# Two adaLN layers on one core: the opening's loads and gate clamps, one rotation in the overlap of the layers, and the loads of the first large feed-forward weights, each put at another place in the order of work

## The chip, the cores and the metric

One core of a Trainium2 chip runs the whole program. The metric is the device time of one execution in microseconds (us). The kernel before was timed in three runs: 1821.15, 1821.19 and 1821.67, median 1821.19. One more execution was profiled.

The names of the profile: PE is TensorE (the matrix products), PEld the loading of its weights, DVE is VectorE, ACT is ScalarE, POOL is GpSimd, SP is SyncE, which here only issues transfers (DMAs). SPq and POOLq rows are DMA issues of those engines. PEclk or "clock" is the share of full speed that TensorE was granted.

## The reference

Eight batches of 512 tokens with 256 features go through two layers. Each layer draws six vectors per batch from a small input c, and uses them to scale and shift a layer norm ahead of an attention and ahead of a feed-forward block, and to gate what is added back:

```python
def layer(x, c, wmod, attn, ffn):                    # twice: L0 and L1
    sa, ca, ga, sb, cb, gb = split6(silu(c) @ wmod)  # per batch, 256 each
    ga = (2 * (ga >= 0) - 1) * maximum(abs(ga), 0.25)   # "clamp"
    gb = (2 * (gb >= 0) - 1) * maximum(abs(gb), 0.25)
    x = x + ga * attn(layernorm(x) * (1 + ca) + sa)
    x = x + gb * ffn(layernorm(x) * (1 + cb) + sb)
    return x

def L0_attn(x):      # 16 heads of 16
    h = rmsnorm(x) * norm_w
    q, k, v = h @ Wq, h @ Wk, h @ Wv
    lin = causal linear attention on taylor(q @ Wqf), taylor(k @ Wkf), v
    win = softmax attention in a window of 64 keys on q, k, v
    return x + concat(lin, win) @ Wout

def L0_ffn(x):
    xr, xk = mixes of x and the token before it (mu_r, mu_k)
    return sigmoid(xr @ W_r) * (square(relu(xk @ W_k)) @ W_v)

def L1_attn(x):      # 16 heads of 16, causal softmax
    Q, K, V = split(x @ w_qkv); Q, K = rope(Q), rope(K)
    return softmax(causal(Q @ K.T / 4)) @ V @ w_proj + b_proj

def L1_ffn(x):       # w1, w2, h1, h2, w3: ternary weights (-1, 0, 1), a scale per output
    h = silu(x @ w1 * s) * (x @ w2 * s)              # 256 -> 1024
    h = gelu(h @ h1 * s); h = gelu(h @ h2 * s)       # 1024 -> 1024, twice
    return h @ w3 * s                                # 1024 -> 256
```

## The kernel before

**The order of the work.** For everything up to the feed-forward block of layer 1 the order is written out by hand. Each piece of work is a small function, entered in a plan with a time by `when(time, what)` (layer 0) or `when1(time, what)` (attention of layer 1). The plan is sorted by time, and the pieces issue their instructions in that order, each to the queue of its own engine; an engine works through its queue in order. So a piece's time sets its place in the queues and nothing else: it waits there until its inputs and its memory are ready, and all that stands behind it on that engine waits too. The unit of time in layer 0 is a step; a batch has 20 steps, and steps from 169 on (the last attention steps and the block after them) count for 0.8. In layer 1 a step counts for 0.603 from its tenth on, and its first falls at 160.6 of layer 0's scale: this stretch, in which the last batches of layer 0 and the first scores of layer 1 stand side by side in the plan, is called the overlap here. Pieces with a negative time are the opening.

**The opening (lines 150 to 310, and 924 to 937).** SP issues the loads: the two c's, x of batch 0, the three slices of layer 0's modulation weights (wm), then Wq, Wk, Wv, wqf, wkf, normw, then layer 1's wm and the rest. `on_every_row` (L228) makes, by products with a c that is spread over all rows (L226), the rows 1+ca, sa and ga for batch 0, all in one PSUM tile; the modulation on DVE (L409, L411) reads the first two, a clamp (L214 to 220) the third. `by_batches` (L235) makes the rows of all batches, `kept_batches` (L246) adds 1 or clamps them, and writes them to `mod_dram`, from where each later batch fetches its rows (`mod_rows`, L124; `fetch_rows`, L386). `mod_features` (L258) makes those of the six vectors that are needed by feature (L266, products with 8 columns), and six DVE instructions copy them out (L271). `folded` (L187) multiplies Wq by Wqf's blocks and Wk by Wkf's, beginning with two transposes on PE (L191). POOL scales Wq, Wk and Wv by normw (L308), and fills constant tiles (memsets, L299 to 310). Batch 0 itself: statistics (L348), `root` and `better` (L327 and L333, the reciprocal root), norm (L364), modulation, sums of squares (L429), a second root, hr (L437), transposes (L452), projections to q and k (L103), products with the folded weights (L467), q's and k's parts (L474 to 487), and the first scores (L545).

**Layer 0 per batch.** Linear scores, window scores, values (L678, L693) and row sums; `finish(b)` (L748) makes the output projection and the feed-forward block. `keys(c)` (L848) projects for one half of the features, and `squared(c)` (L851) takes relu on ACT (L859) into a tile "relu" with the tag "rot" (all but the last batch), and multiplies on DVE into ka (L860).

**Layer 1's first q and k (`rotation`, L1097).** For batch 0 they are made in the overlap, for each of k and q in two chunks of 128 features: `projected` (PE, L103 in the profile's row of such products), `copied` (ACT, to "flat"), `swapped` (DVE, a stream shuffle into a tile "rot", the tag that relu has too), `rotated` three times (POOL, L1119), and `apart` twice (ACT, L1126), which writes the two parts that the scores read. The times stand in a table (L1143 to L1148).

**The feed-forward block of layer 1.** The last pieces of the plan are `gated(f)` and `gate_parts(f, i)` for f from 0 to 7, for batch 0: products (L1454), silu on ACT (L1466), row on DVE (L1469), and a split of row into two parts gh (DVE, L132) and gl (POOL, L133; DVE for the last f). Row has two buffers. Then the program loads a flag and branches: `feed_forward(True)` (L1485) runs if all weights are exactly ternary, which they are here. It opens its own memory pools and issues on POOL sixteen loads (h1 and h2, eight slices of 512 KB each, L1503 to L1507) and one of w3. The large products (L1543) run in groups of 16 per f and batch, 128 x 512 each. Its order within the branch is set by the scheduler of the framework, not by the plan.

**Pools.** The tiles of layer 0 and 1 come from pools with fixed tags and numbers of buffers (`fm`, `atp`, `tok`, `rp`, `wp`; PSUM: `sc`, `mm`). A pool that is closed gives its memory back, and a tile placed there later waits for those that used it.

Of the kernel before, what the change touches and what calls it, by code (L numbers as in the profile page):

```python
# [8 lines left out]
FP = mybir.dt.float32  # L9
BF = mybir.dt.bfloat16  # L10
FR = mybir.dt.float32r
# [6 lines left out]
P = 128  # L18
# [9 lines left out]
PAD = (24, 32)  # L28
# [8 lines left out]
def adaln_two_layers_kernel(ctx: ExitStack, tc: tile.TileContext, t, out):  # L37
# [100 lines left out]
    with ExitStack() as lctx:  # L138
# [3 lines left out]
        atp = lctx.enter_context(tc.tile_pool(name="at0", bufs=2))  # L142
# [10 lines left out]
        xs0, sT, wm = {}, [], []  # L153
        cs = [load(rp, f"c{i}", [P, NC, B], t[f"L{i}_cT"].rearrange("(k p) b -> p k b", p=P)) for i in range(2)]
        xs0[0] = tok.tile([P, NTB, D], FP, name="x", tag="x", bufs=4)
        nc.sync.dma_start(out=xs0[0], in_=t["L0_attn_x"][0].rearrange("(j p) d -> p j d", p=P))
# [14 lines left out]
        wq, wk, wv = (wqkv0[:, :, i * D : (i + 1) * D] for i in range(3))  # L171
        for w, name in ((wq, "L0_attn_Wq"), (wk, "L0_attn_Wk"), (wv, "L0_attn_Wv")):
# [3 lines left out]
        normw = load(rp, "normw", [P, NC], t["norm_w_cols"])  # L176
# [51 lines left out]
        def on_every_row():  # L228

            ps = got0["bc"] = sc.tile([P, 2, T], FP, name="sc", tag="sc")  # L230
            for o, v in ((D, 1), (0, 0)):
                mod_product(ps[:, 0, o : o + D], s_all, 0, v * D, D)
            mod_product(ps[:, 1, :D], s_all, 0, 2 * D, D)
# [12 lines left out]
        def kept_batches(layer, i=1):  # L246
            ps = got0["rows"]
            if i == 0:
                nc.vector.tensor_scalar_add(mod_a[:, 0, :], ps[:B, 0, D:], 1.0)
                nc.vector.tensor_copy(mod_a[:, 1, :], ps[:B, 0, :D])  # L250
            elif layer == 0:
                clamp(mod_a[:, 2:4, :].rearrange("p v d -> p (v d)"), ps[:B, 1, :])
                nc.sync.dma_start(out=mod_dram[:, 0:4, :], in_=mod_a)
            else:
                clamp(mod_b, ps[:B])
                nc.sync.dma_start(out=mod_dram[:, 4:6, :], in_=mod_b.rearrange("p (v d) -> p v d", d=D))

        def mod_features(i):  # L258
            if i == 0:
                got0["f"] = sc.tile([P, 2, T], FP, name="sc", tag="sc")  # L260
            psf = got0["f"][:, 0, : 6 * NC * B].rearrange("p (v c b) -> p v c b", v=6, c=NC)
            layer, v = ((0, 3), (0, 4), (1, 0), (1, 1), (1, 3), (1, 4))[i]
            for c in range(NC):
                w, o = wm[layer][v // 2], v % 2 * D + c * P
                for k in range(NC):
                    nc.tensor.matmul(  # L266
                        psf[:, i, c, :], w[:, k, o : o + P], sT[layer][:, k, :], start=(k == 0), stop=(k == NC - 1)
                    )
            if i == 5:
                for i in range(6):  # L270
                    nc.vector.tensor_scalar_add(modf[:, i], psf[:, i], float(i % 2))  # L271
# [46 lines left out]
        def when(time, what):  # L318
            plan.append((min(time, END0) + STEP0 * max(time - END0, 0.0), len(plan), what))
# [53 lines left out]
        def prepare(b):  # L373
# [3 lines left out]
            def fetch():  # L377
                if b == 0:
                    got0["ga"] = held["bc"] = rp.tile([P, 3, D], FP, name="bc", tag="bc")
                    return  # L380
                xs0[b] = tok.tile([P, NTB, D], FP, name="x", tag="x", bufs=4)
                nc.sync.dma_start(out=xs0[b], in_=t["L0_attn_x"][b].rearrange("(j p) d -> p j d", p=P))
                if b > 1:
                    fetch_rows()

            def fetch_rows():  # L386
                held["bc"] = mod_rows(rp, b, 0, 3, 1)

            when(t0 - 24.5, fetch)
            if b == 1:  # L390
                when(t0 - 22.7, fetch_rows)
# [3 lines left out]
                [t0 - 21.3 + 0.3 * j for j in range(NTB)],  # L395
                t0 - 20.25,
                [t0 - 17.85 + 0.4 * j for j in range(NTB)],
# [3 lines left out]
            row = lambda i: bcast(held["bc"][:, i, :], [P, NTB, D], 1)  # L401
# [74 lines left out]
            def apart(c, which, e):  # L476
                if e == 0:
                    ready[b, c, which] = fm.tile(
                        [P, 2, T], FP, name="q" + which, tag="q" + which, bufs=3 if which == "k" else 2
                    )  # L480
# [462 lines left out]
        def bring(i):  # L943
# [24 lines left out]
            else:  # L968
# [10 lines left out]
                fpool.tile([P, PAD[0]], FP, name="pad0", tag="pad0")  # L979
# [49 lines left out]
        def prepare1(b):  # L1029
# [67 lines left out]
            def rotation(c, which, in_time, at, then, turn, last):  # L1097
# [46 lines left out]
            for c, which, at, begin, then, turn, last in (  # L1144
# [340 lines left out]
    def feed_forward(exact):  # L1485
# [3 lines left out]
        with ExitStack() as fctx:  # L1489
# [6 lines left out]
            if exact:  # L1496
                tok.tile([P, PAD[1]], FP, name="pad1", tag="pad1", bufs=1)
            hp = fctx.enter_context(tc.tile_pool(name=f"hw{exact}", bufs=1 if exact else 3))
            mm = fctx.enter_context(tc.tile_pool(name=f"mm2{exact}", bufs=8, space=PSUM))

            if exact:
                h1 = hp.tile([P, NF, DH], FR, name="h1", tag="h1")
                for dst, name in ((h1, "h1T"), (h2, "h2T")):  # L1503
                    src = t[name].rearrange("(k p) n -> p k n", p=P)
                    for k in range(NF):
                        nc.gpsimd.dma_start(out=dst[:, k, :], in_=src[:, k, :])
                nc.gpsimd.dma_start(out=w3, in_=t["w3T"].rearrange("(k p) n -> p k n", p=P))  # L1507
                full.update(h1T=h1, h2T=h2)
# [187 lines left out]
```

## Time and profile before

| what | us |
|---|---|
| runs, median of 3 | 1821.19 |
| the profiled execution | 1825.46 |
| its span, first to last instruction | 1823.7 |
| PE busy | 1755.0 (96%) |
| DVE busy | 1073.2 (59%) |
| ACT busy | 883.8 (48%) |
| POOL busy | 720.6 (40%) |
| first product on PE | at 7.73 |
| first scores of layer 0 (L545) | at 33.74 |
| first large product (L1543) | at 1177.74 |

How to read it: the profiled execution took 4.27 us more than the median run, 1.76 us of it ahead of or behind the span. Times in the trace are from the span's start. A row of the timeline reads: start, duration, engine, line, operation, output<-inputs, shape, count of instructions that were put together, and in brackets the idle time of the engine before it with what ended it. A row of the waits reads: the waiting engine and line, `<-`, the engine and line that it waited for, total us, count, longest.

Where PE waits longest, by that reading: 7.73 at the start for the first slice of wm; 1.28 at 20.98 for hr; 0.78 at 35.64 and 2.36 at 53.77 behind DVE; 1.22 at 650.74 and 2.39 at 654.79 behind DVE; 1.06 at 677.00 behind ACT; and 7.20 at 1177.74.

### The profile page before, as it was taken

The page shows a single profiled execution, that of the slowest core. Times are in us where ns is not written, and L with a number is a line of the kernel's source. Part 1 is how long each engine was busy: PE and PEld are TensorE (multiplying, and loading weights), DVE is VectorE, ACT ScalarE, POOL GpSimd, SP SyncE. Part 2 cuts the span into 40 slices and gives each one's busy share as a digit, 9 for nine tenths or more (in the row PEclk, how much of TensorE's full clock was granted, in tenths as well). Part 3 has the DMA queues.
Part 4 walks back from the last instruction along what each step waited for, and adds up shares of the span by engine and source line. Part 5 has one row for each costly group of instructions (what it writes and reads, how often), then busy time and mean ns, then how long its engine had stood idle before and what let it go on. Part 6 is the DMA issues. An engine that isn't in the chain of part 4 may idle for free. (4 is left out here: it accounts for less than half of the span.)

```text
span 1823.7 us, 41142 instructions
## 1 busy us (share of the span) xinstructions
PE 1755.0 (96%) x16886; PEld 1200.6 (66%) x16886; DVE 1073.2 (59%) x3712; ACT 883.8 (48%) x1273; POOL 720.6 (40%) x1098
## 2 busy tenths in 40 slices
PE   7899999999999989999999999899999999999998
PEld 4456666665666655544555455588888888888887
DVE  5555574756656556578888887336353554636352
ACT  2766666766667645566666665323221222313221
POOL 4675766768575763456655554400000000000000
PEclk8999999999999999999999999999999999999999
DMA  4100101010001101023121111330000000000000
GB/s 151 37 14 6 37 5 37 5 38 21 24 17 34 40 4 39 1 65 116 50 74 56 56 49 37 122 115 27 1 27 11 17 27 1 27 1 27 0 12 14
DMA packets 42853, 65.59 MB, mean 36 GB/s; under 512 B 4112, under 2 KB 33424, under 8 KB 42656
## 3 DMA queue, kind: packets, MB, share of 16 engines
q1 hardware_dynamic: 37472, 46.62, 8.1%
q0 software_dynamic: 5184, 16.25, 3.0%
q8 instruction: 134, 2.20, 0.5%
q14 instruction: 63, 0.52, 0.1%
HBM read 50.24 MB, written 12.63 MB: 34 GB/s over the span
## 5 line engine op out<-in xcount | busy, mean ns | idle before, releaser
L1543 PE MATMUL mm<-gh,h 128*128 128x512 f32 x1024 | 398.7, 391 | 7.2 <-issue 7.2
L1543 PE MATMUL mm<-gl,h 128*128 128x512 f32 x1024 | 397.9, 390 | 0.0
L1205 DVE CUSTOM_DVE_ANT_0 junk<-sc,cmask 128x256 bf16<-128x256 f32 (+3 forms) x512 | 225.0, 486 | 93.7 <-PE sc L1194 93.3
L132 DVE CAST gh<-row 128x512 fp32r<-128x512 f32 x192 | 80.7, 424 | 265.3 <-ACT row L1589 128.8
L1263 ACT ACTIVATE at<-sc 128x768 f32<-128x768 f32 (+1 forms) x192 | 168.6, 880 | 116.2 <-PE sc L1194 103.0
L1543 PEld LDWEIGHTS mm<-gh,h 128*128 128x128 f32 x1024 | 193.1, 189 | 47.6 <-issue 7.6
L1543 PEld LDWEIGHTS mm<-gl,h 128*128 128x128 f32 x1024 | 193.1, 189 | 40.0
L642 POOL TENSOR_SCALAR_AFFINE_SELECT aw<-aw 64x512 f32<-64x512 f32 (+1 forms) x320 | 168.1, 552 | 101.3 <-ACT aw L632 95.3
L556 ACT ACTIVATE at<-sc 128x768 f32<-128x768 f32 (+1 forms) x192 | 163.9, 883 | 69.3 <-PE sc L545 68.7
L1194 PE MATMUL sc<-k,q 32*128 32x512 f32 (+3 forms) x1024 | 192.6, 473 | 2.2 <-ACT at L1263 2.1
L1252 PE MATMUL sc<-qs,k 32*128 32x384 f32 (+3 forms) x1024 | 190.2, 472 | 1.7 <-DVE qs L1236 1.7
L1267 POOL TENSOR_SCALAR_AFFINE_SELECT at<-at 128x256 f32<-128x256 f32 x256 | 102.9, 414 | 187.5 <-ACT at L1263 187.0
L589 DVE CUSTOM_DVE_ANT_0 junk<-sc,wmask 128x128 bf16<-128x128 f32 x512 | 115.3, 285 | 84.1 <-PE sc L578 84.0
L560 POOL TENSOR_SCALAR_AFFINE_SELECT at<-at 128x256 f32<-128x256 f32 x256 | 103.4, 424 | 112.7 <-ACT at L556 111.8
L1595 ACT ACTIVATE row<-mm,h_s_cols 128x512 f32<-128x512 f32 x64 | 44.0, 687 | 194.7 <-PE mm L1543 191.5
L133 DVE TENSOR_TENSOR gl<-row,gh 128x512 fp32r<-128x512 f32 x185 | 126.8, 689 | 7.2
L1252 PEld LDWEIGHTS sc<-qs,k 32*128 32x128 f32 x1024 | 82.2, 186 | 68.5 <-DVE maxima L1205 35.6
L1589 ACT ACTIVATE row<-mm,h_s_cols 128x512 f32<-128x512 f32 x64 | 43.8, 688 | 153.2 <-PE mm L1543 153.1
L545 PE MATMUL sc<-qm,qk 32*128 32x512 f32 (+3 forms) x1024 | 102.5, 476 | 4.1 <-DVE maxima L589 2.4
L1194 PEld LDWEIGHTS sc<-k,q 32*128 32x128 f32 x1024 | 83.4, 186 | 11.2 <-ACT at L1263 6.9
L1583 ACT ACTIVATE sg<-mm,w_s_cols 128x512 f32<-128x512 f32 x56 | 38.6, 690 | 103.5 <-PE mm L1543 94.6
L578 PE MATMUL sc<-qk,qq 32*64 32x128 f32 x2048 | 77.6, 281 | 5.8 <-issue 4.9
(246 smaller groups left out, 3523.8 us busy)
## 6 DMA issues: line engine op xcount, KB each, us to landing
x_mid<-x SPq DMA_DIRECT2D x16, 512.0 KB, 2.9
x<-x_mid POOLq DMA_DIRECT2D x9, 512.0 KB, 4.3
x<-in_L_attn_x_dram SPq DMA_DIRECT2D x8, 512.0 KB, 4.2
raw<-in_h1T_dram SPq DMA_DIRECT2D x8, 512.0 KB, 3.5
raw<-in_h2T_dram SPq DMA_DIRECT2D x8, 512.0 KB, 3.4
h<-in_h1T_dram POOLq DMA_DIRECT2D x8, 512.0 KB, 7.3
h<-in_h2T_dram POOLq DMA_DIRECT2D x8, 512.0 KB, 11.1
out_dram<-tmp SPq DMA_DIRECT2D x16, 256.0 KB, 2.5
```

What stands on the lines that cost most here:

```text
L133: (rest or nc.vector).tensor_tensor(parts[1], src, parts[0].bitcast(FP), ALU.subtract)
L545: lambda i=i, r=r, kb=kb, n=n, o=o: nc.tensor.matmul(ps[:, i, o : o + n], k[r, e, kb * P : (kb + 1) * P], qm[r, e, kb * P : T], start=True ...
L556: nc.scalar.activation(at, ps[:, :, :o], AF.Square, scale=0.5)
L560: nc.gpsimd.affine_select(out=d, in_=d, pattern=[[0, 2], [1, P]], compare_op=ALU.is_ge, fill=0.0, base=0, channel_multiplier=-1,)
L589: nc.vector.tensor_tensor_reduce(junk, ps[:, i, ii * P : (ii + 1) * P], wmask[:, int(blk > 0), :], -1.0, BIG, ALU.add, ALU.min, maxima[:, ...
L642: nc.gpsimd.affine_select(out=d, in_=d, pattern=[[0, d.shape[1]], [sign, 64]], compare_op=ALU.is_ge, fill=0.0, base=0, channel_multiplier= ...
L1194: nc.tensor.matmul(ps[:, i, o : o + m], q[r, e, qb * P : (qb + 1) * P], k[r, e, :m], start=True, stop=True,)
L1205: nc.vector.tensor_tensor_reduce(junk[:, :m], ps[:, i, o : o + m], got1["cmask"][:, T - m :], -1.0, BIG, ALU.add, ALU.min, maxima[:, NTB * ...
L1252: nc.tensor.matmul(ps[:, i, o : o + m], k[r, e, kb * P : (kb + 1) * P], qs[r, kb * P : T], start=True, stop=True)
L1263: nc.scalar.activation(at, ps[:, :, :o], AF.Exp, scale=0.25)
L1267: nc.gpsimd.affine_select(out=d, in_=d, pattern=[[0, 2], [1, P]], compare_op=ALU.is_ge, fill=0.0, base=0, channel_multiplier=-1,)
L1543: nc.tensor.matmul(ps, w[:, k, col : col + P], part[:, k, :], start=(k == 0 and i == 0), stop=(k == n - 1 and i == len(parts) - 1),)
```

## The change

It has three parts.

**The opening.** x of batch 0 is loaded in two halves, ahead of the c's. normw is loaded ahead of Wq. The third row of `on_every_row`, ga, gets its own PSUM tile, and its clamp, a little sooner, writes an SBUF tile `ga_all`. The first `folded` stands right behind `by_batches(0)`. Four of the six `mod_features` stand sooner. `kept_batches` copies two rows only, and sends them to `mod_dram` at once; the rows ga, gb of layer 0 and of layer 1 are copied by ACT to an SBUF tile `stash`, and are clamped from there at steps 4.05 and 4.95 (before: at -2.75 and 2.6 from PSUM). Batch 1 fetches its rows in two transfers, and its statistics and its norm stand at other times. The six copies to modf become two.

**The overlap.** Of layer 1's batch 0, chunk 1: k's parts go from 161.3 and 162.3 to 166.1 and 166.6; the whole of q goes from 157.7 to 164.3 to 164.85 to 168.7. The norm in layer 1 of batch 1 stands 0.8 sooner; that of batch 2 stands 0.3 sooner, with its four parts closer together.

**The large weights.** k's part tiles move from the pool `fm` to `atp`, and `atp` is closed at step 201.5 of layer 1 by a new piece `first_large`, which opens a pool for h1 there and issues the eight loads of h1 on POOL. The branch loads h2 and w3 only.

```diff
         xs0, sT, wm = {}, [], []
+        xs0[0] = tok.tile([P, NTB, D], FP, name="x", tag="x", bufs=4)
+        for j in range(0, NTB, 2):
+            nc.sync.dma_start(
+                out=xs0[0][:, j : j + 2, :], in_=t["L0_attn_x"][0].rearrange("(j p) d -> p j d", p=P)[:, j : j + 2, :]
+            )
         cs = [load(rp, f"c{i}", [P, NC, B], t[f"L{i}_cT"].rearrange("(k p) b -> p k b", p=P)) for i in range(2)]
-        xs0[0] = tok.tile([P, NTB, D], FP, name="x", tag="x", bufs=4)
-        nc.sync.dma_start(out=xs0[0], in_=t["L0_attn_x"][0].rearrange("(j p) d -> p j d", p=P))
...
-            mod_product(ps[:, 1, :D], s_all, 0, 2 * D, D)
+            got0["f"] = sc.tile([P, 2, T], FP, name="sc", tag="sc")
+            mod_product(got0["f"][:, 1, :D], s_all, 0, 2 * D, D)
...
+        stash = rp.tile([P, NC, T + 1], FP, name="stash", tag="hf")
+        ga_all = rp.tile([P, 2, D], FP, name="ga", tag="ws1")[:, 0, :]
+
+        def kept_batches():
             ps = got0["rows"]
...
+            nc.vector.tensor_scalar_add(mod_a[:, 0, :], ps[:B, 0, D:], 1.0)
+            nc.vector.tensor_copy(mod_a[:, 1, :], ps[:B, 0, :D])
+            nc.sync.dma_start(out=mod_dram[:, 0:2, :], in_=mod_a[:, 0:2, :])
+
+        def copied_batches(layer):
+            nc.scalar.copy(stash[:B, layer, :T], got0["rows"][:B, 1, :] if layer == 0 else got0["rows"][:B])
+
+        def clamped_batches(layer):
+            dst = mod_b if layer else mod_a[:, 2:4, :].rearrange("p v d -> p (v d)")
+            clamp(dst, stash[:B, layer, :T])
+            nc.sync.dma_start(
+                out=mod_dram[:, 2 + 2 * layer : 4 + 2 * layer, :], in_=dst.rearrange("p (v d) -> p v d", d=D)
+            )
...
-                for i in range(6):
-                    nc.vector.tensor_scalar_add(modf[:, i], psf[:, i], float(i % 2))
+                for i in range(2):
+                    nc.vector.tensor_scalar_add(modf[:, i::2], psf[:, i::2], float(i))
...
-                when(t0 - 22.7, fetch_rows)
+                when(t0 - 31.9, fetch_rows)
+                when(t0 - 15.9, fetch_ga)
             ln = normed(
                 when,
                 lambda: xs0[b],
-                [t0 - 21.3 + 0.3 * j for j in range(NTB)],
-                t0 - 20.25,
-                [t0 - 17.85 + 0.4 * j for j in range(NTB)],
+                [t0 - 21.3 + (2.1 if b == 1 else 0.0) + 0.3 * j for j in range(NTB)],
+                t0 - (18.1 if b == 1 else 20.25),
+                [t0 - (17.6 if b == 1 else 17.85) + (0.3 if b == 1 else 0.4) * j for j in range(NTB)],
...
-        for i, at in enumerate((-14.2, -13.65, -12.1)):
+        for i, at in enumerate((-21.85, -13.65, -12.1)):
             when(at, lambda i=i: folded(i))
-        when(-12.0, lambda: kept_batches(0, 0))
-        when(-2.75, lambda: kept_batches(0))
-        for i, at in enumerate((-21.8, -21.7, -10.3, -6.4, -2.7, -2.6)):
+        for i, at in enumerate((-21.8, -21.7, -12.5, -12.4, -10.3, -6.4)):
             when(at, lambda i=i: mod_features(i))
-        when(-11.95, lambda: clamp(got0["ga"][:, 2, :], got0["bc"][:, 1, :D]))
-        when(2.4, lambda: by_batches(1))
-        when(2.6, lambda: kept_batches(1))
+        when(-12.05, lambda: clamp(ga_all, got0["f"][:, 1, :D]))
+        when(-12.0, kept_batches)
+        when(-10.4, lambda: copied_batches(0))
+        when(1.6, lambda: by_batches(1))
+        when(2.05, lambda: copied_batches(1))
+        when(4.05, lambda: clamped_batches(0))
+        when(4.95, lambda: clamped_batches(1))
...
-            early = ((135.5, (138.7, 0.3), 139.75, (142.15, 0.4)), (153.0, (165.0, 0.3), 166.4, (167.0, 0.2)))
+            early = ((135.5, (138.7, 0.3), 139.75, (142.15, 0.4)), (153.0, (164.2, 0.3), 165.6, (166.2, 0.2)))
             usual = (t0 - 37.0, (t0 - 33.6, 1.0), t0 - 29.4, (t0 - 28.6, 0.6))
+            if b == 2:
+                usual = (*usual[:3], (t0 - 28.9, 0.25))
...
-                        ready1[b, c, which] = fm.tile(
+                        ready1[b, c, which] = (atp if which == "k" else fm).tile(
...
-                (1, "k", 0.45, 156.70, 157.2, (157.5, 158.0, 158.6, 159.2), (161.3, 162.3)),
-                (1, "q", 3.45, 157.70, 158.3, (159.9, 160.2, 160.8, 161.4), (163.3, 164.3)),
+                (1, "k", 0.45, 156.70, 157.2, (157.5, 158.0, 158.6, 159.2), (166.1, 166.6)),
+                (1, "q", 3.45, 164.85, 165.3, (165.5, 165.8, 166.3, 166.8), (168.2, 168.7)),
...
+        def first_large():
+
+            atctx.close()
+            hpool = ctx.enter_context(tc.tile_pool(name="ffn_h", bufs=1, side="right"))
+            h1 = full["h1T"] = hpool.tile([P, NF, DH], FR, name="h1", tag="h1")
+            for k in range(NF):
+                nc.gpsimd.dma_start(out=h1[:, k, :], in_=t["h1T"].rearrange("(k p) n -> p k n", p=P)[:, k, :])
+
         when1(187.0, room)
+        when1(201.5, first_large)
...
-                h1 = hp.tile([P, NF, DH], FR, name="h1", tag="h1")
-                for dst, name in ((h1, "h1T"), (h2, "h2T")):
-                    src = t[name].rearrange("(k p) n -> p k n", p=P)
-                    for k in range(NF):
-                        nc.gpsimd.dma_start(out=dst[:, k, :], in_=src[:, k, :])
+                for k in range(NF):
+                    nc.gpsimd.dma_start(out=h2[:, k, :], in_=t["h2T"].rearrange("(k p) n -> p k n", p=P)[:, k, :])
```

More of the change, by code (lines that the diff above doesn't have):

```diff
@@ L27 @@
 BIG = 3.0e38
-PAD = (24, 32)
 def bcast(ap, shape, axis):
@@ L141, in adaln_two_layers_kernel @@
         fm = lctx.enter_context(tc.tile_pool(name="fm0", bufs=1))
-        atp = lctx.enter_context(tc.tile_pool(name="at0", bufs=2))
+        atctx = ExitStack()
+        atp = atctx.enter_context(tc.tile_pool(name="at0", bufs=2))
         sc = lctx.enter_context(tc.tile_pool(name="sc0", bufs=3, space=PSUM))
@@ L171, in adaln_two_layers_kernel @@
         wq, wk, wv = (wqkv0[:, :, i * D : (i + 1) * D] for i in range(3))
+        normw = load(rp, "normw", [P, NC], t["norm_w_cols"])
         for w, name in ((wq, "L0_attn_Wq"), (wk, "L0_attn_Wk"), (wv, "L0_attn_Wv")):
@@ L175, in adaln_two_layers_kernel @@
         wkf = load(rp, "wkf", [P, P], t["Wkf_blocks"])
-        normw = load(rp, "normw", [P, NC], t["norm_w_cols"])
         load_wm(1)
@@ L244, in by_batches @@
                 mod_product(ps[:, i * D : (i + 1) * D], sT[layer], layer, v * D, D)
-        def kept_batches(layer, i=1):
+        stash = rp.tile([P, NC, T + 1], FP, name="stash", tag="hf")
+        ga_all = rp.tile([P, 2, D], FP, name="ga", tag="ws1")[:, 0, :]
+        def kept_batches():
             ps = got0["rows"]
[L248 to L256, printed above, removed]
+            nc.vector.tensor_scalar_add(mod_a[:, 0, :], ps[:B, 0, D:], 1.0)
[9 more added lines that the diff above has]
+            )
         def mod_features(i):
-            if i == 0:
-                got0["f"] = sc.tile([P, 2, T], FP, name="sc", tag="sc")
             psf = got0["f"][:, 0, : 6 * NC * B].rearrange("p (v c b) -> p v c b", v=6, c=NC)
@@ L378, in fetch @@
                 if b == 0:
-                    got0["ga"] = held["bc"] = rp.tile([P, 3, D], FP, name="bc", tag="bc")
                     return
@@ L386, in fetch_rows, with fetch_ga @@
             def fetch_rows():
-                held["bc"] = mod_rows(rp, b, 0, 3, 1)
+                if b > 1:
+                    held["bc"] = mod_rows(rp, b, 0, 3, 1)
+                    return
+                held["bc"] = rp.tile([P, 3, D], FP, name="bc", tag="bc")
+                nc.sync.dma_start(out=held["bc"][:, 0:2, :], in_=mod_dram[b, 0:2, :].partition_broadcast(P))
+            def fetch_ga():
+                nc.sync.dma_start(out=held["bc"][:, 2, :], in_=mod_dram[b, 2, :].partition_broadcast(P))
             when(t0 - 24.5, fetch)
             if b == 1:
-                when(t0 - 22.7, fetch_rows)
+                when(t0 - 31.9, fetch_rows)
+                when(t0 - 15.9, fetch_ga)
             ln = normed(
@@ L400, in prepare @@
             )
-            row = lambda i: bcast(held["bc"][:, i, :], [P, NTB, D], 1)
+            row = lambda i: bcast(held["bc"][:, i, :] if b else ga_all, [P, NTB, D], 1)
             def modulated(i):
@@ L477, in apart @@
                 if e == 0:
-                    ready[b, c, which] = fm.tile(
+                    ready[b, c, which] = (atp if which == "k" else fm).tile(
                         [P, 2, T], FP, name="q" + which, tag="q" + which, bufs=3 if which == "k" else 2
@@ L977, in bring @@
                 full["h"] = [fpool.tile([P, NC, T], FR, name="h" + e, tag="h" + e) for e in "hl"]
-                fpool.tile([P, PAD[0]], FP, name="pad0", tag="pad0")
+                fpool.tile([P, 24], FP, name="pad", tag="pad")
                 for name in ("w1_s_cols", "w2_s_cols", "h1_s_cols", "h2_s_cols"):
@@ L1495, in feed_forward @@
             tok = fctx.enter_context(tc.tile_pool(name=f"tok2{exact}", bufs=2 if exact else 1))
-            if exact:
-                tok.tile([P, PAD[1]], FP, name="pad1", tag="pad1", bufs=1)
-            hp = fctx.enter_context(tc.tile_pool(name=f"hw{exact}", bufs=1 if exact else 3))
+            if not exact:
+                hp = fctx.enter_context(tc.tile_pool(name="hw", bufs=3))
             mm = fctx.enter_context(tc.tile_pool(name=f"mm2{exact}", bufs=8, space=PSUM))
             if exact:
-                h1 = hp.tile([P, NF, DH], FR, name="h1", tag="h1")
-                for dst, name in ((h1, "h1T"), (h2, "h2T")):
-                    src = t[name].rearrange("(k p) n -> p k n", p=P)
-                    for k in range(NF):
-                        nc.gpsimd.dma_start(out=dst[:, k, :], in_=src[:, k, :])
+                for k in range(NF):
+                    nc.gpsimd.dma_start(out=h2[:, k, :], in_=t["h2T"].rearrange("(k p) n -> p k n", p=P)[:, k, :])
                 nc.gpsimd.dma_start(out=w3, in_=t["w3T"].rearrange("(k p) n -> p k n", p=P))
-                full.update(h1T=h1, h2T=h2)
+                full["h2T"] = h2
                 gs = [full["g"], [gp.tile([P, NF, T], FR, name="g" + e, tag="g" + e) for e in "hl"]]
```

## The prediction

> **What bounds the kernel now.** I read the engines' share and slices first, then the windows with the granted clock, then the waits and the timeline of the stretches that the diff touches.
>
> ```profile
> PE 1755.0 (96%) x16886; PEld 1200.6 (66%) x16886; DVE 1073.2 (59%) x3712; ACT 883.8 (48%) x1273; POOL 720.6 (40%) x1098
> PE   7899999999999989999999999899999999999998
> ```
>
> TensorE is busy 96%, and no multiplication is removed. So the change can win only the time in which PE stands (61 us by the gaps between its instructions, 7.73 of it before its first) and the time in which it runs at half clock. The windows show where that is (columns: sum, busy PE, PEld, DVE, ACT, POOL, granted clock, DMA share, GB/s):
>
> ```profile
> 0.00:10.00 10.00, 2.27 (x6) 1.85 (x7) 3.33 (x22) 3.81 (x7) 8.10 (x17) 1.00 0.69 236
> 20.00:30.00 10.00, 9.03 (x24) 5.67 (x25) 4.69 (x14) 1.17 (x2) 4.99 (x3) 0.55 0.12 42
> 30.00:40.00 10.00, 9.22 (x41) 5.74 (x40) 6.96 (x23) 3.67 (x7) 0.00 (x0) 0.79 0.10 22
> 650.00:660.00 10.00, 6.87 (x46) 3.71 (x48) 4.40 (x12) 2.72 (x4) 5.78 (x8) 0.68 0.03 10
> 1170.00:1180.00 10.00, 2.80 (x8) 1.93 (x7) 6.52 (x20) 2.27 (x3) 6.75 (x11) 0.79 1.03 318
> ```
>
> All three places of the change show: the opening, the overlap of the layers near 650, and the start of the feed-forward near 1175. In the trace's clock record the half-clock stretches there are 18.7 to 29.0, 35.8 to 42.6, 653.6 to 660.5 and 1175.9 to 1182.7 us. PE work at half clock costs half of that time.
>
> **Part 1, the first large weights (h1).** Before, POOL issues h1's eight transfers behind its last gl and behind the branch, and PE's first feed-forward product waits for the first slice:
>
> ```profile
> 1170.85 1.27 POOL L133 TENSOR_TENSOR gl<-row,gh 128x512 fp32r<-128x512 f32 x1 [1.43 <-DVE gh L132]
> 1171.37 0.75 DVE L1469 SCALAR_TENSOR_TENSOR row<-sc,w_s_cols,sg 128x512 f32<-128x512 f32 x1 [0.60 <-ACT sg L1466]
> 1172.74 4.31 POOL L1506 DMA_DIRECT2D h<-in_h1T_dram  x8 [0.63 <-DVE gh L132]
> 1177.74 0.77 PE L1543 MATMUL mm<-gh,h 128*128 128x512 f32 x1 [7.20 <-issue]
> ```
>
> The page calls that wait "issue"; it begins at 1170.54, with PE already past the branch, and ends as the first slice lands, 4.7 after its issue. The same eight issues move on POOL between gl of f=1 (1155.71 to 1157.01) and gl of f=2 (1159.54). They wait there only for the last products that read the closed pool, which end near 1151.5, so they run 1157.0 to 1161.3. The slices need 1.28 each (512 KB at the 410 GB/s of before), so the last lands near 1157 + 4.7 + 7 x 1.28 = 1170.7. Gl of f=2 goes from 1159.54 to 1161.3; behind it stand only the other gl's, and DVE's row of f=4, the first that reuses its tile, comes at 1163.26: gl of f=2 is done at 1162.6. What is late next is DVE's row of f=7, which frees the PSUM: its end, 1172.12, plus 0.2. PE starts at 1172.3 instead of 1177.74: 5.4. The gap left is 1.8; the nearest lone gap (1.57 at 293.56) was followed by no half clock, so the stretch 1175.9 to 1182.7, of which PE worked 4.96 after 1177.74, gives 2.48 more. The h2 transfers now queue behind the last gl on DVE (1173.3), land by some 1190 and are needed after eight f of 3.63 us, at 1201. I take -7.7. Bounds: 0 (another wait at the branch takes the place), and -7.2 - 2.5 = -9.7 (no gap left).
>
> **Part 2, the overlap.** The rotation of q (layer 1, batch 0, chunk 1) holds POOL's L1119 in three parts, the last behind a ws product and four selects. Its tile "rot" is also the tile of relu (L859):
>
> ```profile
> ACT relu L859 <- POOL flat L1119: 6.8, 1, 6.8
> PE mm L725 <- DVE ka L860: 2.4, 1, 2.4
> PE mm L725 <- DVE rows L741: 1.2, 1, 1.2
> ...
> 652.12 1.26 POOL L1119 TENSOR_TENSOR flat<-flat,rot 128x512 f32<-128x512 f32 x1
> 653.41 0.60 ACT L859 ACTIVATE relu<-mm 128x512 f32<-128x512 f32 x1 [6.85 <-POOL flat L1119]
> 654.79 1.12 PE L725 MATMUL mm<-ident,ys 128*128 128x128 f32 x4 [2.39 <-DVE ka L860]
> ```
>
> Relu held ACT for 6.85 us, ka on DVE came after it, and PE stood 2.39 behind ka. After the move relu waits only for k's rotation, done at 642.58; so the 2.39 go, and about half of the 1.22 before (DVE's rows are late since xk and xr take 1.0 to 1.76 beside POOL's rotation, and 0.75 alone at 733.72). Without these gaps the stretch 653.6 to 660.5 should run at full clock: PE worked 5.7 of it after 654.79, so 2.85. Together 2.39 + 0.6 + 2.85 = 5.8. The moved instructions: two sets of projections on PE, unchanged; one copy, a shuffle (0.75), three POOL products (1.28 each, 3.9) and four ACT copies (0.8). POOL has an idle 9.20 before 667.40 for the first product; the others queue behind L759 (2.40) and six selects (2.59 and after), so q is ready near 675 and its last part near 677. The scores that read it come near 690: some 13 us of cover. If that is gone, each us late is a us of PE, plus a half-clock stretch. The norm of batch 1 comes 0.8 steps sooner and shares ACT, which idles 1.21 and 1.94 there. The norm of batch 2 is packed closer at 720 to 728, where ACT is busy 9.09 of 10: +-1.5. I take -5.5. Bounds: -1 (the half clock stays, and the moved work gives back what the gaps gave) and -9 (1.22, 2.39, 2.85, and the gaps of 1.07 and 0.68 near 676 and 661, and 0.8 of the norm).
>
> The half-clock stretches here last 6.8 or 10.2 us and follow several gaps close together. The Trainium skill (TensorE: Matmul & The Clock Gate, Part 1) gives one idle window of about 3.4 us as what throttles again; here 1.22 and 2.39 with 1.66 of work between were enough. By the rule the gap left in part 1 is too short as well, so the sum is the same at full clock; but in part 2 the gaps would have cost only themselves, and the sum would be 2.85 smaller.
>
> **Part 3, the opening.** SP issues x's two halves before the c's, and normw ahead of Wq: one DMA more in the opening. The c's (0.95 us of issue) are passed, so the wm transfers start about 1.0 sooner.
>
> ```profile
> 7.73 4.89 PE L226 MATMUL sc<-wm,sall 128*128 128x256 f32 x12 [7.73 <-DMA wm<-in_L_wmod_dram]
> 12.66 1.23 DVE L409 SCALAR_TENSOR_TENSOR h<-sc,h 128x1024 f32<-128x1024 f32 x1 [1.05 <-PE sc L226]
> 18.35 0.49 DVE L196 COPY wT<-mm 128x128 f32<-128x128 f32 x2 [1.52 <-PE mm L191]
> 20.98 2.11 PE L452 MATMUL mm<-ident,hr 128*128 128x128 f32 x8 [1.28 <-DVE hr L437]
> ```
>
> PE starts near 6.7. The modulation on DVE now needs 8 of the 12 products (the third has its own PSUM tile): 6.7 + 8 x 0.49 + 0.2 = 10.8 (the twelve took 4.89 at a clock that was low until 11.9, so I give the first ones 0.49, above their mean of 0.41), against 12.66: 1.9 sooner. DVE's 1.52 wait at 18.35 goes (those transposes now run first). So hr starts near 20.56 - 1.9 - 1.5 = 17.1. One set of modulation products, 1.71, leaves the way from hr to q and the scores, and DVE's clamp of ga comes ahead on it with some 0.4: the first scores come 3.5 + 1.7 - 0.4 = 4.8 before 33.74. If POOL's memsets hold DVE (root at 19.21 took 1.12 instead of 0.17, ending with the memset of 19.36 to 20.31), hr is no sooner and 1.3 is left. The clamps that left PE waiting 0.78 at 35.64 leave too, as does the 2.36 at 53.77 (DVE's clamp of 47.64 to 51.94). They come back as two sets of four at steps 4 to 5, 2.7 us each: from the maxima of step 3 to qf, DVE then has 2.7 + 1.87 + 2.7 + 0.69 = 8.0 against PE's 7.1 less what PE is ahead, a new stall of some 2.7, at most 4.3. Batch 1's rows take a second DMA on SP; modf's six DVE instructions become two (-0.4, hidden). Sum -4.8 - 0.8 - 2.4 + 2.7 = -5.3; I take -5. Bounds: with memsets and the long stall -1.3 - 3.2 + 4.3 = 0; and -9 with the half clock of 35.8 to 42.6 (3.4) gone also.
>
> The row 49.67 to 51.94 (an STT of 2.27 against 0.68 elsewhere, ended as POOL's L413 ended its first at 51.40) shows DVE held by POOL. The skill (SBUF — State Buffer, "SBUF: two separate sides") says the loser of the shared port waits for the whole instruction: it speaks against moving clamps to SBUF sources (stash) beside POOL. By it the eight clamps would lose up to 1.6 each.
>
> **The sum.** -7.7 - 5.5 - 5 = -18.2. The profiled execution took 1825.46 (1823.7 its span), so a profile like it would take 1807.3; the median of the runs is 1821.19, 4.27 lower, so 1803.
>
> **The rivals.**
> (a) The opening is given back: memset hold and clamp stall, 0 for part 3: 1821.2 - 13.2 = 1808. For: the two held rows above. Against: PE has 1.8 us of cover at steps 4 to 5.
> (b) The first weights win nothing, since PE's "issue" wait was the branch itself: 1821.2 - 10.5 = 1811. Against: PE was past the branch at 1167.45.
> (c) More half clock goes (35.8 to 42.6: 3.4; 725.3 to 735.5: 5.1): 1803 - 8.5 = 1795. Against: the second one has its own gaps (1.71 and 0.66) behind ACT.
> (d) Slower: DVE held by POOL in the opening. Place: batch 1's modulation on POOL (L413 to L417, 2.3 to 2.55 each) against the clamps and copies of steps 4 to 5, each held 2.27 - 0.68 = 1.6 as in the row at 49.67. It decides from 11 held instructions on (11 x 1.6 = 18); there are 8 clamps and 4 copies, 19, and a half-clock stretch of 10.2 (5.1) after the stall: 1803 + 24 = 1827. Against: POOL has few such products per batch.
> (e) It doesn't do what it says: the first transfers wait on the closed pool and reach memory no sooner, q is moved without freeing the tile: part 3 alone, 1816.
>
> **How the numbers follow.** What the measurement can tell from no change I put at 0.2%, 3.6 us. Chances: the forecast 0.52, (a) 0.20, (b) 0.06, (c) 0.12, (d) 0.05, (e) 0.05. Each but (d) is faster; of (e) and (a) I give 0.03 to no change: faster 0.92, same 0.03, slower 0.05. The likeliest gives 1803. Own range 1798 to 1808; (a) and most of (c) widen it to 1794 to 1813, which leaves out the rest of (b) and (c), (d) and (e).
>
> **What would show it.** Right: L1543 begins some 1.8 us after L1454 ends, and its 512-wide products are at 0.39 from the start; L859 no longer waits for L1119 and 650 to 660 has clock 1.00; L545 begins near 29. Wrong: L1543 still waits 5 or more; a DVE stall over 4.3 ahead of qf; a new stretch of half clock near 50 to 60 or 690, which would add 3.4 to 5.1.

## The result, and the profile after

The changed kernel took 1814.76 us (median of 7 runs, 1810.34 to 1819.95) against 1821.37 (7 runs of before, 1820.35 to 1826.94): ratio 0.9955, interval [0.9940, 0.9971]. By the ratio that is 8 us faster, between 5 and 11; the two medians differ by 6.6. The prediction said 1803, between 1794 and 1813. The profiled execution took 1810.34, its span 1808.6.

The changed kernel's shares and its windows (columns as before: sum, busy PE, PEld, DVE, ACT, POOL, granted clock, DMA share, GB/s):

```profile
PE 1742.7 (96%) x16886; PEld 1191.8 (66%) x16886; DVE 1079.5 (60%) x3708; ACT 887.3 (49%) x1276; POOL 722.1 (40%) x1098
...
0.00:10.00 10.00, 2.27 (x6) 1.86 (x7) 3.90 (x27) 3.81 (x7) 5.48 (x15) 1.00 0.77 244
50.00:60.00 10.00, 4.96 (x52) 1.72 (x42) 8.64 (x38) 3.13 (x6) 2.96 (x6) 0.66 0.22 69
650.00:660.00 10.00, 9.32 (x53) 6.20 (x54) 6.63 (x26) 4.17 (x9) 1.75 (x3) 1.00 0.01 2
1160.00:1170.00 10.00, 8.21 (x36) 6.47 (x35) 6.91 (x18) 2.11 (x3) 5.75 (x9) 1.00 0.85 264
```

Two of the three places are mended: 650 to 660 and the start of the feed-forward run at full clock. The opening has a new hole: between 50 and 60 PE is busy 4.96 of 10, where it was 7.64 before, and the clock is 0.66 there. The same window of the kernel before:

```profile
50.00:60.00 10.00, 7.64 (x80) 3.17 (x78) 9.82 (x47) 5.32 (x9) 6.53 (x8) 1.00 0.18 56
```

The first large weights, in the timeline of the changed kernel:

```profile
1149.75 4.32 POOL L1500 DMA_DIRECT2D h<-in_h1T_dram  x8
1154.02 1.37 POOL L132 TENSOR_TENSOR gl<-row,gh 128x512 fp32r<-128x512 f32 x1
...
1164.17 0.75 DVE L1489 SCALAR_TENSOR_TENSOR row<-sc,w_s_cols,sg 128x512 f32<-128x512 f32 x1 [0.60 <-ACT sg L1486]
1165.12 0.47 PE L1568 MATMUL mm<-gh,h 128*128 128x512 f32 x1 [1.78 <-issue]
```

The issues stand where they were expected, PE's wait is 1.78 instead of 7.20, and it ends 0.2 after DVE's row of f=7, as the prediction had it; the profile itself calls the wait "issue". The products take 0.39 from the second on.

The overlap, in the same kernel's timeline:

```profile
644.68 0.60 ACT L875 ACTIVATE relu<-mm 128x512 f32<-128x512 f32 x1 [2.75 <-PE mm L102]
646.66 0.69 DVE L876 TENSOR_TENSOR ka<-mm,relu 128x512 f32<-128x512 f32 x1
647.41 0.66 PE L741 MATMUL mm<-ident,ys 128*128 128x128 f32 x4 [0.36 <-DVE ka L876]
```

Relu waits for its own product now, and the 2.39 of PE behind ka are 0.36.

The opening, in the same timeline:

```profile
7.73 4.32 PE L229 MATMUL sc<-wm,sall 128*128 128x256 f32 x12 [7.73 <-DMA wm<-in_L_wmod_dram]
17.52 3.97 DVE L453 TENSOR_SCALAR hr<-h,rr 128x256 f32<-128x256 f32 x4
17.87 1.80 POOL L319 MEMSET vo<- 128x2048 f32 x1
19.61 0.94 POOL L319 MEMSET vs<- 128x1024 f32 x1
...
44.96 5.00 POOL L429 TENSOR_TENSOR h<-h,bc 128x1024 f32<-128x1024 f32 x2 [1.13 <-issue]
45.17 2.57 DVE L222 TENSOR_SCALAR clamps<-stash 8x512 f32<-8x512 f32 x1
47.77 2.73 DVE L223 SCALAR_TENSOR_TENSOR mod<-clamps 8x512 f32<-8x512 f32 x1
53.43 0.41 DVE L222 TENSOR_SCALAR clamps<-stash 8x512 f32<-8x512 f32 x1
53.87 0.68 DVE L223 SCALAR_TENSOR_TENSOR mod<-clamps 8x512 f32<-8x512 f32 x1
54.48 0.67 DVE L490 COPY qf<-mm 128x512 f32<-128x512 f32 x1
55.30 3.94 PE L701 MATMUL mm<-at,vo 128*32 128x512 f32 x32 [5.04 <-DVE qf L490]
```

Hr took 3.97 beside POOL's memsets; four such instructions took 1.14 before. Two clamps took 2.57 and 2.73 beside the two products of L429, where the same lines of the other set, with no such product beside them, take 0.41 and 0.68. Everything behind them on DVE is late, and PE stands 5.04 us, with a half-clock stretch from 51.7 to 58.5 behind it.

**The clock has to be read with every time here.** The profiled executions differ by 15.1 us, the medians by 6.6. Each run lists its mean granted clock, and (1 - clock) x span, called lost below (known to 1.8 us, since the clock has three digits), follows the times closely: over 67 runs of before the time rises by 0.74 us per us lost, with a correlation of 0.95, and lost runs from 20.0 to 34.8; over 17 runs of after by 0.84 (0.96), lost 12.7 to 25.5. In all 13 profiles every half-clock stretch lasts 3.41, 6.83 or 10.24 us, but for one at the end of each span, and the same kernel has more or fewer of them in different runs. Lost also counts half of the time that PE stands within such a stretch, so time less lost is a fair measure only between kernels with a similar lost. So the profile of after, with 12.7 lost, shows its luckiest case, and that of before, with 27.4, one a little worse than its mean.

### The profile page after: what moved, and what is told of

Its sections match the earlier page's. It is cut to its first block, busy times and chain, and to the rows that moved or that the text cites. A ratio compares the mean times of both kernels' runs of the same rounds, so it can differ in the third digit from the quotient of the medians.

```text
span 1808.6 us, 41155 instructions
## 1 busy us (share of the span) xinstructions
PE 1742.7 (96%) x16886; PEld 1191.8 (66%) x16886; DVE 1079.5 (60%) x3708; ACT 887.3 (49%) x1276; POOL 722.1 (40%) x1098
## 4 chain that ended last, share of the span: by engine, by line
PE 56%; ACT 3%; POOL 3%; DVE 2%; issue 1%; DMA 0%; ACTq 0%; POOLq 0%; DVEq 0%
PE mm L1568 31%; PE sc L1272 7%; PE mm L1306 4%; PE mm L1631 3%; PE mm L1124 2%; PE mm L1364 2%; PE mm L1182 2%; PE sc L1214 1%; ACT at L1283 1%; POOL flat L1139 1%; PE sc L1474 1%; POOL at L1287 1%; PE mm L1248 1%; PE mm L798 1%; ACT k L1146 1%
## 5 line engine op out<-in xcount | busy, mean ns | idle before, releaser
L648 ACT ACTIVATE aw<-sc 128x1024 f32<-128x1024 f32 (+1 forms) x64 | 62.2, 972 | 43.7 <-PE sc L638 42.3
```

## The experiments

Eleven runs followed: both kernels again, and nine variants. The table gives the mean of each, the mean lost, the rest (time less lost) and the median with the ratio to the runs of before on the same chip. "before" are 67 runs, "after" 17, the others 5 to 12; a mean is uncertain by about 1 us, a rest by 0.2 to 0.8 (one standard error). The variants ran on three chips (e3, e4; e5 to e8; e9 to e11), on which the rest of before is 1797.7, 1797.5 and 1798.7.

| kernel | mean | lost | rest | median | ratio, interval |
|---|---|---|---|---|---|
| before | 1824.0 | 26.1 | 1797.9 | 1823.4 | |
| after | 1816.2 | 19.5 | 1796.7 | 1815.7 | 0.9955 [0.9940, 0.9971] and 0.9959 [0.9941, 0.9977] |
| e4 large weights alone | 1816.3 | 22.1 | 1794.2 | 1816.3 | 0.9959 [0.9943, 0.9974] |
| e3 after, no opening | 1815.2 | 18.7 | 1796.5 | 1815.9 | 0.9955 [0.9938, 0.9972] |
| e11 overlap alone | 1823.1 | 23.4 | 1799.8 | 1823.0 | 0.9992 [0.9982, 1.0001] |
| e5 clamps moved | 1810.7 | 18.1 | 1792.7 | 1809.4 | 0.9930 [0.9912, 0.9949] |
| e6 and memsets | 1809.9 | 17.4 | 1792.5 | 1809.7 | 0.9929 [0.9912, 0.9946] |
| e7 after, overlap mended | 1816.0 | 21.6 | 1794.4 | 1815.9 | 0.9961 [0.9948, 0.9974] |
| e8 e6 and e7 | 1811.9 | 21.7 | 1790.2 | 1812.1 | 0.9940 [0.9922, 0.9957] |
| e9 e6, cover kept | 1809.7 | 17.8 | 1791.9 | 1809.5 | 0.9920 [0.9906, 0.9933] |
| e10 e9, one norm back | 1808.5 | 18.1 | 1790.4 | 1808.5 | 0.9912 [0.9899, 0.9924] |

**Both kernels again.** No edit.

> The kernel before once more, for its clock. I call lost = (1 - granted clock) x span. Theory A (the half-clock stretches come and go from run to run, and the two profiled executions were by chance one with much and one with little): the runs lie on time = 1798 +- 1.5 + lost, with lost between 20 and 30 us, and a profile with a span near 1820 shows the same gaps of PE as before (1.2 and 2.4 near 650, 7.2 near 1175) but other half-clock stretches. Theory B (something else than the clock varies): the runs do not lie on one line against lost, and the gaps differ.

> The changed kernel once more. Theory A: time = 1796 +- 1.5 + lost, lost between 12 and 24, median near 1815; the gaps of the first profile stay (5.0 before L701 near 55, 1.1 at hr, 1.8 before the large products), the half-clock stretches are others. Theory B: a gap that was not in the first profile explains the slower runs.

Before: rest 1797.7 with a standard deviation of 1.1, lost 21.8 to 34.7, beyond the 30 expected. A second profile, with a span of 1819.9, has the same large gaps (1.22 and 2.40 near 650, 1.71 near 714, 7.02 before the large products). Its half-clock stretches stand at the same places: 3.4 instead of 10.2 near 128, and near 720 the same 10.2 in two pieces of 3.4 and 6.8. Its span is 3.8 shorter, and by the clock record 3.4 less is lost. After: rest 1797.1 with a standard deviation of 1.0, lost 12.7 to 25.5 and median 1817.43, both a little beyond what was expected. Its second profile fell on the same light case as the first, so which stretches the other runs add was not seen. Theory A stands: the spread follows the clock, and between the two profiles of before no gap differs by enough to make it. That the stretches would be at other places was wrong for both.

**The parts.** e3 is after with the opening of before; e4 is before with `first_large`, its pool and k's tiles in `atp`; e11 is before with the new times of the overlap.

> The kernel before with the early issue of h1 alone (and the pool of k's parts that makes room for it). The gap before the large products 1.8 instead of 7.2 and no half clock there in any run: 5.4 + 2.5 less than before: 1813.5 in the median. If that half clock were by chance too, 5.4 only: 1816. If another wait took its place: 1821.

Mean 1816.3 against 1824.5 of before on the same chip. Against all runs of before it is 7.7 less. PE's wait is 1.78, with no half clock behind it in the profile (a stretch of 3.4 stands at 1136.7). The median, 1816.34, is the number expected if the half clock were by chance too; but the runs of before on the same chip were 2.5 slower as well, so the difference, 7.5 in the medians and 8.2 in the means, is the one forecast with the half clock. And that half clock is not by chance in the profiles at hand: the three that have a gap of 6.8 to 7.2 there have 6.83 us of it, and the ten with 1.78 have none. So the part did what was predicted, and it alone is about all that the whole change wins.

> The change without its opening part: the opening of before, with the overlap and the large weights of after. Theory A says the opening part costs at full clock (the stretch up to 444 us is 3.7 shorter in the profile, of which the clock alone gives 6.3: so +2.6): time less lost is 1793.5, the median 1811 to 1814. Rival: the opening part wins its 3.7 in every run: median near 1818.

Mean 1815.2: 1.0 below after, 1.1 below e4. Neither side was right. By the rest the opening part costs 0.2 and not 2.6, and it does not win 3.7 either. The difference in the means, +1.0, is uncertain by about 1.5: a gain of 5 is excluded, a loss is not shown.

> The kernel before with the overlap's part alone. If the parts add: as without the opening against the large weights alone, 1 below before in the mean, with lost 3.4 below before's 26.3 and time less lost 2.3 above its 1797.6. My prediction's value was 5.5 below: 1818. Rival: the overlap wins more where the large weights do not follow it, 3 or more below before.

Mean 1823.1 against 1824.1 of before on the same chip, rest 1.1 above it and lost 2.0 below: with the interval up to 1.0001, hardly a gain. It agrees with the 1.1 between e3 and e4, so the overlap is worth the same with the large weights and without. For the opening there is no such second measurement: -7.7 (e4 from before), -1.1 (e3 from e4) and +1.0 (after from e3) make up the -7.8 of the whole by their definition.

**The clamps.**

```diff
-        when(4.05, lambda: clamped_batches(0))
-        when(4.95, lambda: clamped_batches(1))
+        when(1.2, lambda: clamped_batches(0))
+        when(12.4, lambda: clamped_batches(1))
```

> The changed kernel, but the two sets of clamps at steps 1.2 and 12.4 instead of 4.05 and 4.95. Theory C (DVE's clamps stand beside POOL's L429 products and make the 5.0 stand of PE before L701): that gap falls under 1, the half clock of 51.7 to 58.5 goes, time less lost is 4 to 5 below the changed kernel's 1796.7, the median 4 to 7 below its median. Rival: the values' copies (L543) or qf hold PE anyway, the gap stays over 2 and the time is the same.

The timeline of e5, at the places of the lines above:

```profile
35.71 0.62 DVE L222 TENSOR_SCALAR clamps<-stash 8x512 f32<-8x512 f32 x1
36.36 0.87 DVE L223 SCALAR_TENSOR_TENSOR mod<-clamps 8x512 f32<-8x512 f32 x1
45.45 4.92 POOL L429 TENSOR_TENSOR h<-h,bc 128x1024 f32<-128x1024 f32 x2 [1.13 <-issue]
46.77 0.69 DVE L490 COPY qf<-mm 128x512 f32<-128x512 f32 x1 [1.05 <-PE mm L102]
50.69 2.36 PE L701 MATMUL mm<-at,vo 128*32 128x512 f32 x32
```

With no clamp beside L429 the copies (L543) and qf come 7.7 us sooner (46.77 against 54.48), L701 waits for nothing, and no half clock follows there. The rest falls by 4.0, the mean by 5.5. This is shown: the clamps' place ahead of qf made the hole. That it is the hold and not the mere length of the clamps is worked out from the rows: in the profile of after the set beside L429 took 6.4 and the other 2.4, and the copies behind it 1.62 against 1.00 here. Without the hold qf would have come some 4.6 sooner, and about 0.4 of the 5.04 would be left, an estimate; no run keeps the clamps there and moves L429. The time was 1809.4, faster than both kernels.

**The memsets.** POOL's three later memsets are put ahead of the scaling of Wq, Wk and Wv.

```diff
-        for w in (wq, wk, wv):
...
         for v in (vswap[0], vones[1], vswap[1]):
             nc.gpsimd.memset(v, 1.0)
+        for w in (wq, wk, wv):
...
```

> As e5, and POOL's three later memsets stand before its scaling of Wq, Wk, Wv. Theory C': hr took 3.97 instead of 1.14 beside those memsets; now 1.2, and the first scores come 1.5 to 2.8 sooner than at 32.6: time less lost 1.5 to 2.8 below e5. Rival: the scaling, later by the memsets, makes the projections (L102 near 24.6) wait and gives it back: same as e5.

The timeline of e6:

```profile
18.42 1.14 DVE L453 TENSOR_SCALAR hr<-h,rr 128x256 f32<-128x256 f32 x4
19.04 2.32 PE L275 MATMUL sc<-s,wm 128*128 128x8 f32 x16
21.21 1.95 PE L468 MATMUL mm<-ident,hr 128*128 128x128 f32 x8
24.52 6.64 PE L102 MATMUL mm<-hT,wqkv 128*128 128x512 f32 x8
```

Hr takes 1.14 again. But it did so in e5 too, with the memsets unmoved; there the row ahead of hr, one of the second root, was held in its stead:

```profile
17.27 2.87 DVE L346 TENSOR_SCALAR rt<-rt 128x4 f32<-128x4 f32 x1
17.42 1.79 POOL L319 MEMSET vo<- 128x2048 f32 x1
19.17 0.94 POOL L319 MEMSET vs<- 128x1024 f32 x1
20.37 1.14 DVE L453 TENSOR_SCALAR hr<-h,rr 128x256 f32<-128x256 f32 x4
```

So it is in all profiles of the new opening: with the memsets unmoved either hr takes 3.97 (after) or L346 takes 2.6 to 2.9 (e2, e5, e7), and hr is done at 21.5 to 21.7; with them moved (e6, e8, e9, e10) L346 takes 0.17 and hr is done at 19.3 to 19.6. The memsets were what held DVE. But nothing is won (rest 1792.5 against 1792.7): PE comes to hr's transposes at 21.21, after 32 modulation products that stand ahead of them, and runs at half clock from 20.2 to 30.5 here, where e5 had 22.0 to 28.8. The first scores come at 33.90, 0.8 later than in e5. The rival's outcome, for another reason than its own: the projections did not wait for the scaling.

**The overlap.** e7 and e8 put q's projection and copy back, and the two norms:

```diff
-                (1, "q", 3.45, 164.85, 165.3, (165.5, 165.8, 166.3, 166.8), (168.2, 168.7)),
+                (1, "q", 3.45, 157.70, 158.3, (165.5, 165.8, 166.3, 166.8), (168.2, 168.7)),
...
-            early = ((135.5, (138.7, 0.3), 139.75, (142.15, 0.4)), (153.0, (164.2, 0.3), 165.6, (166.2, 0.2)))
+            early = ((135.5, (138.7, 0.3), 139.75, (142.15, 0.4)), (153.0, (165.0, 0.3), 166.4, (167.0, 0.2)))
-            if b == 2:
-                usual = (*usual[:3], (t0 - 28.9, 0.25))
```

What they are to mend is seen in e3, which has the overlap of after. Its timeline:

```profile
630.03 1.52 DVE L364 TENSOR_SCALAR hr<-x,rr,off 128x256 f32<-128x256 f32 x2
631.28 1.09 PE L812 MATMUL mm<-ident,hr 128*128 128x128 f32 x6 [1.06 <-DVE hr L364]
...
659.44 1.17 DVE L337 TENSOR_SCALAR rt<-rt 128x4 f32<-128x4 f32 x1
660.54 2.37 POOL L759 TENSOR_TENSOR ws<-L_attn_Wout,br 128x1024 f32<-128x1024 f32 x1
660.65 2.28 DVE L338 TENSOR_TENSOR rr<-rr,rt 128x4 f32<-128x4 f32 x1
665.33 1.13 PE L1196 MATMUL sc<-k,q 32*128 32x512 f32 x4 [1.15 <-DVE maxima L1207]
...
712.55 1.00 ACT L1265 ACTIVATE at<-sc 128x1024 f32<-128x1024 f32 x1
713.61 1.20 PE L1196 MATMUL sc<-k,q 32*128 32x384 f32 x4 [1.49 <-ACT at L1265]
```

In e4, with the old overlap, hr takes the same 1.53 beside POOL's rotation, but PE has q's projection (1.88) to do meanwhile. With the projection moved away PE stands 1.06. The root of batch 1's norm, 4 elements wide, takes 2.28 beside L759 (2.37 long), and PE stands 1.15 behind the maxima. The exponential L1265 now stands behind a part of batch 2's norm, and PE stands 1.49, and then 0.51 and 0.62 more behind the next two. The part removed 1.05 and 2.18 near 650 (e4's numbers), of which 0.35 is left, and four short waits for hr of batch 2's norm near 718, 1.22 together. Over the whole stretch that lies between the same products in both, e4 first, then e3:

```profile
484.91:749.00 264.09, 249.86 (x3263) 153.15 (x3263) 154.69 (x646) 155.76 (x233) 154.93 (x239) 0.97 0.08 24
485.20:746.47 261.27, 246.64 (x3263) 150.76 (x3263) 155.93 (x646) 155.88 (x233) 154.69 (x239) 0.99 0.08 24
```

PE stands 14.23 us there in e4 and 14.63 in e3: the new gaps ate all that the removed ones gave. What this stretch of e3 is shorter by, 2.8, is PE's busy time at a higher clock.

> The changed kernel, but q's projection and copy (chunk 1) at their old times, only its shuffle, POOL products and parts later, and the norms of batches 1 and 2 at their old times. Theory D (the overlap's gaps were removed and three new ones made: 1.06 before L828 since the projection no longer covers hr, 1.15 before L1214 since the norm's root meets POOL's q rotation, 1.49 before L1214 behind ACT since batch 2's norm is packed): the first and third go; time less lost 2 to 3 below the changed kernel. Rival: the gaps reappear elsewhere in the overlap, no difference within 1.

All three gaps went from their places, and the rest fell by 2.3 as expected. But lost rose by 2.1, and the mean is that of after. The timeline of e7:

```profile
669.89 0.58 ACT L371 ACTIVATE h<-x,off,rr 128x256 f32<-128x256 f32 x1
670.38 0.56 ACT L1190 COPY vo<-mm 128x512 f32<-128x512 f32 x1
671.00 1.00 PE L1246 MATMUL mm<-ident,maxima 128*128 128x128 f32 x4 [2.39 <-ACT vo L1190]
```

Batch 1's norm, back at its old time, stands on ACT ahead of the copy vo, PE waits 2.39 instead of 1.13, and a half-clock stretch runs from 671.2 to 678.0. In e4 the norm stands ahead of vo too, and the gap is 1.06; but there q's POOL products are done, while in e7 four rows of its root (L344 to L347) take 2.78 beside POOL's products instead of 1.45. So by the rows it is the old norm and the late q together.

> e6 and e7 together. If theories C, C' and D hold and add: time less lost 8 to 10 below the changed kernel's 1796.7, median 1804 to 1808, faster than both kernels. Rival: median within 2 of e6.

Rest 6.5 lower, not 8 to 10, and the same 2.4 gap with the same stretch behind it (668.1 to 674.9): 2.4 slower in the median than e6.

> e6 (clamps and memsets moved), and q's projection and copy (chunk 1) back at their old times, both norms as changed. Theory D, its first part: the gap of 1.05 before L828 goes and nothing else; time less lost 1 below e6's 1792.5, lost as in e6 (17.4), since the 2.4 gap before L1246 that e7 and e8 had came from batch 1's norm at its old time: median 1808 to 1810. Rival: that gap came from the projection's place: it is there again, with a half clock behind it, and the median is near e8's 1812.

Right in its gaps: the 1.05 is gone, the one before vo's reader (L1248 here) is 1.13, no rival's gap, though 3.4 of half clock stand behind it, as in e5. PE stands 13.90 in the stretch between the same products as above, against 14.90 in e6. The rest is 0.6 lower, less than the uncertainty; against before on its own chip it is 6.8 lower, where e6 is 5.0 lower on its chip.

> As e9, and batch 2's norm at its old time, batch 1's still 0.8 sooner. Theory D, its last part: the 1.49 gap behind ACT near 712 goes, but the gaps of 0.99 and 0.62 and the half clock of 6.8 that e7 and e8 show near 720 to 730 come back: time less lost 0.5 to 1.5 below e9, lost 1.7 to 3.4 above it: same or 2 slower. Rival: batch 2's packed norm costs its 1.49: 1.5 faster than e9.

The 1.49 went. Of the gaps that should have come back only one of 0.65 before L828 is there, though a half-clock stretch of 10.2 stands at 716; lost over all runs is 18.1. The rest falls by 1.5, the median by 1.0, which the intervals of e9 and e10 don't tell apart. PE stands 12.29 in the same stretch, 1.6 less than in e9. So batch 2's packed norm costs its gap in the profiles, as the rival said; that the time falls by as much isn't settled. e10 has the lowest time of all, 1808.5, and e5, e6 and e9 are within 1.2 of it: any of them beats both kernels.

## Why the prediction was wrong, by its own steps

The whole was forecast at -18.2 and came at -7.8 (means of all runs). Part 1 gave what was forecast; the 10.4 that are missing are 4.4 of part 2 and 6 of part 3.

**Part 1, the large weights, -7.7: right.** Measured -7.7 (e4), with the wait of 1.8 that was named and no half clock. That both numbers end on the same tenth is luck: the measured one is uncertain by about 0.8.

**Part 2, the overlap, -5.5: wrong in size (-1.1, uncertain by about 1.4).** The removed gaps were priced rightly (2.39 to 0.36; the stretch at 653.6 is gone). What failed is the cost of the moved instructions, put at nothing: "two sets of projections on PE, unchanged" counted their length and not what they covered. The projection had hidden hr (1.06). "The norm of batch 1 ... shares ACT" named the wrong engine: it shares DVE with POOL's products, and its root was held 2.28 (a gap of 1.15). Packing batch 2's norm, put at "+-1.5", cost 1.49 and two smaller gaps. In sum PE stands 0.4 longer in e3 than in e4; the 1.1 that was won came from the clock (lost 22.1 to 18.7). The bound of -1 was close to the truth, for another reason than its own: it had the half clock stay, and the half clock went.

**Part 3, the opening, -5: nothing won (+1.0, uncertain by about 1.5).** Four steps failed.
- "The c's ... are passed, so the wm transfers start about 1.0 sooner": x passes the c's, but the c's still stand ahead of wm, and x has one issue more. The issues of wm start 0.5 later (lines below), and PE's first product is at 7.73 again (7.60 to 7.88 in the eight profiles with the new opening, 7.34 to 7.98 in the five with the old).
- The memsets: the hold was written as a bound, not as the value. It came in every profile with the changed order of POOL. In that order two memsets stand behind the scaling of the weights where before one did; that normw, loaded sooner, changed the order is likely, and no run shows it.
- "The first scores come ... 4.8 before 33.74": they came at 32.62, and at 32.62 to 33.90 in the eight profiles, against 32.86 to 34.23 with the old opening. The sum let the scores follow hr. In e6, with hr done at 19.56, PE still came to its transposes at 21.21: the modulation products that the change put ahead of them (32 instead of 16) were not in the sum. The set that left the way further on was there replaced by a wait of 1.00 for ACT (qq).
- "A new stall of some 2.7, at most 4.3": 5.04. The clamps were summed at their undisturbed 2.7 a set, though the row at 49.67 in the profile before had shown one held by L413; two were held here by L429 (the same line in the changed kernel), by 2.2 and 2.0. Rival (a) was this, with its price, as it put it, "0 for part 3".

The issues of wm, in the kernel before and in the changed one:

```profile
2.32 1.53 SPq L166 DMA_DIRECT2D wm<-in_L_wmod_dram  x3
2.83 1.49 SPq L169 DMA_DIRECT2D wm<-in_L_wmod_dram  x3
```

**Half clock.** Each stretch was priced as if tied to the gap before it, and the sum was set against the median without saying that the same kernel loses from 20 to 35 us by the clock from run to run, with a spread of 13 to 15 us in lost for both kernels. Of rival (c) the stretch at 35.8 did go, but the one at 51.7 came in its place. A prediction whose parts are 1 to 8 us had to have a wider range for that alone. The Trainium skill ("TensorE: Matmul & The Clock Gate", Part 1) says that the activity window runs free, so that the number of slow products at a kernel's start differs between runs. What it says of the start is seen here over the whole kernel; that the window is the reason, no run here shows.

**The rival that it would be slower** (DVE held by POOL in eleven instructions) had the right mechanism: two clamps and hr were held, for 7.0 us together (2.2, 2.0 and 2.8), too few to turn the sign.

## What to carry to other kernels

A moved piece of work takes its cover with it: list what waited while it ran, and what then stands bare. Before placing DVE instructions, look at what POOL does in the same microseconds; an undisturbed duration is no price there. And before counting on an input that comes sooner, list what stands ahead of its reader in the reader's own queue. Where runs of one kernel differ by 10 us in the granted clock, compare times at equal clock, and judge parts by running them alone.

## What the runs showed of the hardware

A memset on POOL, which reads nothing, held DVE instructions with one tensor input from SBUF: hr (128x256) took 3.97 for four against 1.14, or a row of the root, 4 elements wide, 2.87 against 0.17; neither did with the memsets moved. Rows of 4 elements were also held as long as POOL's products beside them (2.28 beside 2.37, 1.17 beside 1.27 in e3). The Trainium skill ("SBUF — State Buffer", "SBUF: two separate sides") says that `tensor_scalar`, which hr is, can enter a mode that uses both ports of DVE and then contends with GpSimd. Whether hr ran in that mode, no run here shows.

The length of a gap alone did not tell whether half clock follows. Gaps of 2.39 that stand alone (e7, e8) had 6.8 us of it behind them, and the 1.78 before the large products had none in any of the ten profiles that have it. But the gap of 0.89 near 1135, the same in all thirteen, had a stretch of 3.4 beginning at it in four (e4, e5, e9, e10) and none in nine; and the one of 1.60 near 125 (with one of 1.0 ahead of it), which the list ahead of the prediction leaves out, had 3.4, 6.8 or 10.2 in twelve and none in e7.
